# Two ends of an attention kernel written as lists of single-engine steps, with all leaf sums of weights on GpSimd

## The chip, the cores and the metric

The kernel runs on one core of a Trainium2 chip. The metric is the device time of one execution in microseconds. The kernel before took 1024.07 us, the median of 3 runs (1023.55 to 1025.17).

## The reference

The inputs are 64 blocks of 128 tokens with 512 channels in float32, a mask, a bias for each of 16 heads and the weights. What is computed is attention with one shared key/value head, a layer norm ahead of it and one behind it, and a residual:

```
xn   = layernorm(x, g_in)
q    = (xn @ Wq) * 64**-0.5        # 16 heads of 64
k, v = split(xn @ Wkv)             # one head of 64, shared
k, v = a null key and a null value (from cond) put in front of k and v
sim  = q k^T + bias, -max where the key is later than the query or masked
out  = softmax(sim) v              # joined to 1024 channels
x    = x + layernorm(out @ Wo, g_out)
```

## The kernel before

The instructions of each engine stand in the order in which the Python functions are called: the tile framework adds the semaphores, but moves nothing. Each engine takes its own queue in order, and so does SyncE (SP), which issues nearly all DMAs. So the order of the calls is the schedule.

The work goes in cycles of two blocks (`cycle(c)`, 28 of them, c from 2 to 29), each a fixed table of steps (`EVEN` and `ODD`). A cycle makes the q projection of blocks ahead, softmax and values of two blocks, and the output projection and layer norm of older ones. At its end `region_mm(c)` puts the scores of the next two blocks and the values of these two on TensorE. The scores of the first of the two go into the PSUM bank `s`, which the values need next: so TensorE waits there for VectorE to add the scores to the bias tile (`scores_add`, the rows `s<-ps,s`).

q projections and output projections are done with seven products instead of eight (sums of quarters of the operands are formed first); half of the q products go one level deeper. The sums of weights for that level are the "leaf sums": `leaf_weights(k, j)` for five leaves k and four sums j, 20 adds or subtracts of 128x256 elements in all, made once. The sums j = 1, 2 and 4 write a tile of their own (`wL`); j = 3 overwrites part of the weights (`wq` or `wS`), and so may only run once the products that need those weights are done. The table of cycle 2 is the first to use them.

Ahead of cycle 2 stands a part written by hand: loads, the norm of the first 16 blocks, scaling of `wq` by the gain (`weights_q`), the transposes of tokens on TensorE (`norm_T`, tile `pxT`), q products of the first group in full (`q_half`, tile `pq`), the keys and values (`kv_mm`, `kv_out`, tile `kT`), a transposed copy of the values (`vt`, written by VectorE, sent to DRAM as `vd`), a DMA that copies the keys to the upper half of the partitions (`kT<-kT`), bias tiles on GpSimd (`bias_add`, 128x1552), then `region(-1)`, the first seven-product q projections (`q_one`), `region(0)`, and `second()`, which is cycle 1 and ends with `region(1)`. Nine leaf sums run on GpSimd there, eleven on VectorE: six in a row in `second()`, five of the kind that overwrites, in ones and twos, shortly ahead of `region(1)`.

Behind cycle 29 a second hand-written part finishes the last six blocks: `scores_lower`, `scores_upper`, `exps`, `scale`, `blocks_T` and `values_one` for blocks 60 to 63, three sets of seven output products (`out_one`), the last layer norms (`pair_stats`, `pair_center`, `pair_scale`) and the stores.

The calls that both VectorE stretches come from:

```
        for j in (1, 2, 4):
            leaf_weights(1, j, nc.vector)
            leaf_weights(5, j, nc.vector)
```

Of the kernel before, what the change touches and what calls it, by code (L numbers as in the profile page):

```python
# [17 lines left out]
def kernel(  # L18
# [63 lines left out]
    P = 128  # L82
# [236 lines left out]
    def norm_T(m):  # L319
        g, t = divmod(m, GB)  # L320
        if t == 0:
            xT[g] = gp.tile([P, GB, KC, N], FP, tag="xT", name=f"xT_{g}")
        xh = xs.pop(m)
        pt = ps_w.tile([P, KC, P], FP, tag="w", name=f"pxT_{m}")
        for kc in range(KC):
            nc.tensor.transpose(pt[:, kc, :], xh[:, kc * P : (kc + 1) * P], ident)
        nc.scalar.copy(xT[g][:, t], pt)

# [107 lines left out]
    def q_part(g, c, h):  # L436

        f = c % NF
        return qT[g, f // FH, h][:, f % FH, :, :, c // NF, :]

    def q_half(c, h, at=None):
        if c == 0 and h == 0:
            for fp in range(2):
                q_tile(0, fp)
        tag = at or ("XY"[c % 2] if h else "ac"[c % 2])
        pq = (ps_q if tag in "ac" else ps_y).tile([P, HT], FP, tag=tag, name=f"pq_{c}_{h}")
        two = slice(2 * h, 2 * h + 2)
        for kc in (2, 0, 3, 1):
            nc.tensor.matmul(
                pq,  # L450
                wq[:, kc, c * P : (c + 1) * P],
                xT[0][:, two, kc, :],
                start=(kc == 2),
                stop=(kc == 1),
            )
        nc.scalar.copy(
            q_part(0, c, h),
            pq.rearrange("p (t i q) -> p t i q", t=2, i=NQ),
        )

    def q_first(f, k, tag):

        pool = {"a": ps_q, "c": ps_q, "X": ps_y, "Y": ps_y, "s": ps_s, "w": ps_w}[tag]
        if f == 0 and k == 1:
            for fp in range(2):
                q_tile(0, fp)
        product(0, f, k, pool, tag, start=k in (1, 2, 5))
        o = {
            1: (f, 0),
            2: (f, 0),  # L470
            6: (f, 1),
            7: (HC + f, 1),
            4: (HC + f, 0),
            5: (HC + f, 1),
            3: (f, 1),
        }[k]
        o = q_part(0, *o)
        if k in (2, 3, 5):
            nc.vector.tensor_tensor(o, by_block(tag), o, ALU.add)
        else:  # L480
            nc.scalar.copy(o, by_block(tag))
# [469 lines left out]
    def out_sum(p, k):  # L951

        if k == 0:
            yS[p] = bp.tile([P, HC, N], FP, tag="yS", name=f"yS_{p}", bufs=1)
        h11, h12 = oT[p][:, lo_c], oT[p][:, hi_c]
        h21, h22 = oT[p + 1][:, lo_c], oT[p + 1][:, hi_c]
        o, l, m, op = (
            (yS[p], h21, h22, ALU.add),
            (h11, yS[p], h11, ALU.subtract),
            (h21, h22, h11, ALU.subtract),  # L960
            (h12, h12, h11, ALU.subtract),
        )[k]
        nc.gpsimd.tensor_tensor(o, l, m, op)  # L963

    def out_product(p, k, pool, tag, start=True):
        key = "y" + tag
        if start:
            prod[key] = pool.tile([P, HE], FP, tag=tag, name=f"py{tag}_{p}_{k}")
        a, b = oT[p], oT[p + 1]
        h, w = {  # L970
            1: lambda: (a[:, lo_c], e11),
            2: lambda: (a[:, hi_c], e21),
            3: lambda: (a[:, hi_c], e22),
            4: lambda: (b[:, hi_c], wT[:, 2]),
            5: lambda: (yS[p], wT[:, 0]),
            6: lambda: (a[:, lo_c], wT[:, 1]),
            7: lambda: (b[:, lo_c], e12),
# [122 lines left out]
    def q_one(c, k, h):  # L1100
        i = 2 * c + 4 + h
        g, f = divmod(i, GB)
        if k == 1 and f % FH == 0:
            q_tile(g, f // FH)
        if k == 1:
            product(g, f, 1, ps_q, "a")
            keep("a", "p1")
        elif k == 2:
            product(g, f, 2, ps_w, "w")
            q_out(g, f, lo_t, "w", "p1")  # L1110
        elif k == 5:
            product(g, f, 5, ps_q, "c")
        elif k == 6:
            product(g, f, 6, ps_q, "a", start=False)
            keep("a", "u2")
        elif k == 7:
            product(g, f, 7, ps_q, "a", start=False)
            keep("a", "u3")
            q_out(g, HC + f, hi_t, "c", "u3")
        elif k == 3:  # L1120
            product(g, f, 3, ps_q, "c", start=False)
            q_out(g, f, hi_t, "c", "u2")
        else:
            product(g, f, 4, ps_q, "a", start=False)
            q_out(g, HC + f, lo_t, "a")

# [22 lines left out]
    def out_one(p, k, dve=False):  # L1149
        if k == 3 and at_end:  # L1150
            out_add(p, 3)
        out_mm(p, k)
        if k in (1, 6, 7) or (k == 4 and not at_end):
            out_copy(p, k, dve)
        if k == 4 and at_end:
            out_part(p + 1, 0, "w", "yu3")
        elif k == 3 and at_end:
            o = y_half(p, 1)
            nc.vector.tensor_tensor(o, prod["yw"], o, ALU.add)
        elif k in (2, 3, 7):  # L1160
            out_add(p, k)

# [8 lines left out]

    def region(c):
        n0, n1 = 2 * c + 2, 2 * c + 3
        region_mm(c)
        scores_add(n0, 1)
        scores_add(n0, 0)
        if c < 0:
            scores_max(n0, 0)
            scores_max(n0, 1)
        scores_add(n1, 0)  # L1180
        scores_add(n1, 1)

    def key_values(m):
        if m < B:
            kv_out(m, kv_mm(m))

    def second():
        b0, b1, n0, n1 = 2, 3, 4, 5
        p, m = 0, 12
        load_mask(2)  # L1190
        load_x(m)
        values_out(p, (0, 2))
        scores_max(b1, 0)
        scores_max(b1, 1)
        values_out(p + 1, (0, 2))
        scores_max(b0, 0)
        tokens_in(2)
        q_one(1, 1, 0)
        q_one(1, 5, 0)
        values_out(p, (1, 3))  # L1200
        values_out(p + 1, (1, 3))
        out_sum(p, 0)
        scores_max(b0, 1)
        q_one(1, 2, 0)
        exps(b0, 0, 0, 2)
        q_one(1, 6, 0)
        exps(b0, 0, 2, 8)
        out_one(p, 1)
        mask_neg(1)
        out_sum(p, 1)  # L1210
        for j in (1, 2, 4):
            leaf_weights(1, j, nc.vector)
            leaf_weights(5, j, nc.vector)
        rinv(b0, 0)
        q_one(1, 7, 0)
        out_one(p, 2)
        exps(b0, 1, 0, 6)
        norm_stats(m)
        q_one(1, 4, 0)
        load_x(m + 1)  # L1220
        q_one(1, 3, 0)
        scale(b0, 0)
        q_one(1, 1, 1)
        q_one(1, 2, 1)
        exps(b0, 1, 6, 8)
        exps(b1, 0, 0, 6)
        norm_stats(m + 1)
        rinv(b0, 1)
        scale(b0, 1)
        key_values(8)  # L1230
        out_sum(p, 3)
        q_one(1, 6, 1)
        exps(b1, 0, 6, 8)
        norm_apply(m)
        out_sum(p, 2)
        exps(b1, 1, 0, 4)
        tokens_T(m)
        out_one(p, 6)
        rinv(b1, 0)
        q_one(1, 5, 1)  # L1240
        exps(b1, 1, 4, 8)
        load_x(m + 2)
        nc.tensor.addr_align(256, offset=120, max_nops=16)
        scale(b1, 0)
        token_sum(2, 1)
        token_sum(2, 2)
        out_one(p, 5)
        norm_apply(m + 1)
        blocks_T(b0)
        rinv(b1, 1)  # L1250
        q_one(1, 7, 1)
        tokens_T(m + 1)
        out_one(p, 7)
        scale(b1, 1)
        q_one(1, 3, 1)
        blocks_T(b1)
        out_one(p, 4)
        bias_add(n0)
        leaf_weights(3, 3, nc.vector)
        load_x(m + 3)  # L1260
        load_res(p + 1)
        q_one(1, 4, 1)
        leaf_weights(4, 3, nc.vector)
        bias_add(n1)
        out_one(p, 3)
        leaf_weights(2, 3, nc.vector)
        leaf_weights(1, 3, nc.vector)
        leaf_weights(5, 3, nc.vector)
        load_res(p)
        leaf_sums(2, 1)  # L1270
        leaf_sums(2, 5)
        region(1)
# [419 lines left out]


    nc.vector.tensor_scalar(gin8, gin, DH**-0.5, None, ALU.mult)
    keep_busy(14)
    load_second()
    norm_stats(0)
    norm_stats(1)
    norm_apply(0)
    norm_T(0)  # L1700
    norm_apply(1)
    for kc in (2, 0, 3, 1):
        weights_q(kc, 0)
    norm_T(1)
    keep_busy(2)
    causal()
    norm_stats(2)
    norm_stats(3)
    norm_apply(2)
    norm_apply(3)  # L1710
    q_half(0, 0)
    weights_kv()
    weights_q(2, 1)
    q_half(1, 0)
    norm_T(2)
    weights_q(3, 1)
    norm_T(3)
    load_x(11)
    weights_q(0, 1)
    norm_stats(4)  # L1720
    weights_q(1, 1)
    norm_stats(5)
    q_half(2, 0)
# [319 lines left out]
```

## Time and profile before

| | |
|---|---|
| median of 3 runs | 1024.07 us |
| profiled execution, its own time | 1022.62 us |
| its span, first to last instruction | 1020.8 us |
| TensorE (PE) busy | 1002.5 us, 98% |
| VectorE (DVE) busy | 908.3 us, 89% |
| GpSimd (POOL) busy | 834.8 us, 82% |
| ScalarE (ACT) busy | 677.6 us, 66% |
| mean granted TensorE clock | 0.996 |

TensorE is busy for almost the whole span, so only its idle time, and time at a lower clock, can be saved without taking work away. A timeline row reads: start in us, duration in us, engine, line, operation, out<-in, shape, and in brackets the idle time before it with what ended it. In a row with several instructions (x4) the duration is that of the whole stretch. Ends of matmuls are modelled, so from row to row the starts are what tells. A table by stretches gives busy time and, as PEclk, the share of the full TensorE clock that was granted.

### The profile page before, as it was taken

To read this page: it belongs to the slowest core of one execution; us is meant where nothing else is said; L and a number is where in the kernel's file an instruction comes from. 1 tells how busy PE (TensorE), PEld (TensorE's weight loads), DVE (VectorE), ACT (ScalarE), POOL (GpSimd) and SP (SyncE) were. 2 spreads that over 40 slices of the span, in tenths; PEclk is the share of its full clock that TensorE was granted. 3 is DMA by queue.
4 is the path that set the end of the run, shared out by engine and by line. 5 is a ranking of instruction groups with operands and counts; after the bars stand their busy time and mean duration, and the time that the engine had idled before them with its cause. 6 is when DMAs were issued, how large, how long until landed. Compare 5 with 4: busy or idle time off the path is not lost. (4 is left out here: it accounts for less than half of the span.)

```text
span 1020.8 us, 32742 instructions
## 1 busy us (share of the span) xinstructions
PE 1002.5 (98%) x12440; PEld 901.8 (88%) x12440; DVE 908.3 (89%) x2151; ACT 677.6 (66%) x2826; POOL 834.8 (82%) x819
## 2 busy tenths in 40 slices
PE   9998999999999999999999999999999999999997
PEld 8887899999999999999999999999999999999876
DVE  7787899898998989999898998989999898888898
ACT  2654766668766668766668766668766668756591
POOL 3798879789797997979789796997979789696874
PEclk9999999999999999999999999999999999999999
DMA  6541242333424325342333424325342332421212
GB/s 220 158 128 32 61 120 85 105 88 105 128 83 130 86 64 138 94 120 84 106 88 104 129 82 127 85 69 137 96 119 84 107 86 84 119 65 43 73 34 103
DMA packets 70293, 101.37 MB, mean 99 GB/s; under 512 B 27744, under 2 KB 31328, under 8 KB 68320
## 3 DMA queue, kind: packets, MB, share of 16 engines
q1 hardware_dynamic: 69008, 97.83, 34.1%
q8 instruction: 123, 2.02, 0.9%
q10 hardware_dynamic: 1104, 1.05, 0.3%
q14 instruction: 58, 0.48, 0.2%
HBM read 63.19 MB, written 33.55 MB: 95 GB/s over the span
## 5 line engine op out<-in xcount | busy, mean ns | idle before, releaser
L821 ACT ACTIVATE s<-s,nmax 128x129 f32<-128x129 f32 (+1 forms) x1024 | 374.7, 377 | 3.5 <-DVE nmax L812 3.5
L755 POOL TENSOR_TENSOR s<-biasp,mneg 128x1552 f32<-128x1552 f32 x64 | 206.0, 3232 | 11.7 <-DVE sb L857 9.8
L842 POOL TENSOR_TENSOR s<-s,rinv 128x512 f32<-128x512 f32 (+1 forms) x128 | 188.4, 1481 | 23.2 <-DVE rinv L838 21.5
L821 ACT ACTIVATION_READ_ACCUMULATOR s<-s,nmax 128x1 f32 x1024 | 205.4, 201 | 0.0
L576 DVE TENSOR_TENSOR qT<-pl,qT 128x128 f32<-128x128 f32 (+1 forms) x420 | 127.6, 331 | 43.3 <-PE pl L573 38.3
L930 ACT ACTIVATE oT<-poY,nv 128x256 f32<-128x256 f32 x58 | 29.2, 503 | 202.9 <-PE poY L890 190.8
L807 DVE TENSOR_TENSOR s<-ps,s 128x256 f32<-128x256 f32 (+2 forms) x224 | 122.3, 599 | 15.1 <-PE ps L771 14.6
L980 PE MATMUL pyX<-wo,oT 128*128 128x256 f32 x512 | 121.6, 380 | 0.5 <-ACT kyu L1013 0.5
L812 DVE TENSOR_REDUCE nmax<-s 128x8 f32<-128x1032 f32 (+1 forms) x128 | 119.9, 949 | 0.1
L980 PE MATMUL pyX<-wT,oT 128*128 128x256 f32 x488 | 115.6, 380 | 0.7 <-POOL oT L963 0.7
L857 DVE STREAM_TRANSPOSE sb<-s 128x1536 f32<-128x1536 f32 x64 | 112.6, 1759 | 1.8 <-POOL s L842 1.8
L963 POOL TENSOR_TENSOR yS<-oT 128x512 f32<-128x512 f32 x32 | 41.0, 1281 | 82.4 <-ACT oT L930 81.6
L980 PEld LDWEIGHTS pyX<-wo,oT 128*128 128x128 f32 x512 | 92.7, 190 | 12.1 <-issue 1.1
L980 PEld LDWEIGHTS pyX<-wT,oT 128*128 128x128 f32 x488 | 88.3, 190 | 10.9 <-POOL oT L963 1.1
L771 PE MATMUL ps<-kT,qT 64*64 64x128 f32 (+1 forms) x4096 | 93.7, 245 | 0.7 <-issue 0.7
L771 PEld LDWEIGHTS ps<-kT,qT 64*64 64x64 f32 x4096 | 85.6, 134 | 5.8 <-issue 2.4
L890 PE MATMUL pos<-sb,vr 32*64 32x128 f32 (+1 forms) x1792 | 82.1, 324 | 4.1 <-DVE s L807 3.9
L890 PE MATMUL poY<-sb,vr 32*64 32x128 f32 x720 | 75.3, 351 | 0.0
L890 PE MATMUL poX<-sb,vr 32*64 32x128 f32 x960 | 74.4, 302 | 0.0
L980 PE MATMUL pyw<-wo,oT 128*128 128x256 f32 x280 | 66.4, 380 | 0.1
L890 PEld LDWEIGHTS pos<-sb,vr 32*64 32x64 f32 x1792 | 60.8, 131 | 4.8 <-DVE s L807 4.2
L890 PEld LDWEIGHTS poX<-sb,vr 32*64 32x64 f32 x960 | 56.2, 132 | 5.9 <-issue 5.2
(180 smaller groups left out, 2681.3 us busy)
## 6 DMA issues: line engine op xcount, KB each, us to landing
res<-in_x_dram SPq DMA_DIRECT2D x64, 256.0 KB, 3.0
out_dram<-y SPq DMA_DIRECT2D x58, 256.0 KB, 2.1
x<-in_x_dram SPq DMA_DIRECT2D x224, 64.0 KB, 2.0
xd<-xb SPq DMA_DIRECT2D x14, 1024.0 KB, 4.6
xT<-xd SPq DMA_DIRECT2D x56, 256.0 KB, 6.3
vr<-vd SPq DMA_DIRECT2D x64, 128.0 KB, 3.6
x<-in_x_dram SPq DMA_DIRECT2D x8, 256.0 KB, 4.9
vd<-vt SPq DMA_DIRECT2D x32, 64.0 KB, 4.2
```

Source lines behind the costliest of these rows:

```text
L576: nc.vector.tensor_tensor(o, p, o, ALU.add)
L755: nc.gpsimd.tensor_tensor(S[b], biasp, mneg[:, t].unsqueeze(1).broadcast_to([P, R8, ROW]), ALU.add,)
L771: nc.tensor.matmul(to[r][i * DH : (i + 1) * DH, f, :], qT[g, f // FH, t // GH][rows, f % FH, t % GH, NQ - 1 - i if hf else i], kT[g][rows, ...
L807: nc.vector.tensor_tensor(sv, ps, sv, ALU.add)
L812: nc.vector.tensor_reduce(nmax[b][:, hf], S[b][:, :, WITH_NULL[hf]], AX.X, ALU.max, negate=True)
L821: nc.scalar.activation(row, row, AF.Exp, bias=nmax[b][:, hf, k : k + 1], accum_out=rsum[b][:, hf, k : k + 1],)
L842: nc.gpsimd.tensor_tensor(sv, sv, rinvs.pop((b, hf)).unsqueeze(2).broadcast_to([P, R8, sv.shape[2]]), ALU.mult,)
L857: nc.vector.transpose(sb.rearrange("p j e q -> p e j q"), S[b][:, :, 1 : ROW - 1].rearrange("p e (j k) -> p e j k", k=Q),)
L890: nc.tensor.matmul(po[s][rows, half], vr[g][quad(s), j, t, :], sb[quad(s), slots, r * NF : (r + 1) * NF, :], start=start, stop=True, skip_ ...
L930: nc.scalar.activation(o, pos[b][s], AF.Identity, bias=nv2)
L963: nc.gpsimd.tensor_tensor(o, l, m, op)
L980: nc.tensor.matmul(prod[key], h[:, c, :], w[:, c, :], start=(start and c == 0), stop=(c == HC - 1), skip_group_check=not start,)
```

## The change

Both hand-written parts become lists of steps, `FRONT` (from the first norm to the end of cycle 1) and `TAIL` (from cycle 29 to the end), run through a table of functions `act`. Helpers that issued to several engines are split, so that each step belongs to one engine: `q_half` becomes `qh` (products) and `qhc` (copy), `norm_T` becomes `xTt` and `xTc`, `q_one` becomes `q`, `qk`, `qo` and `qc`, the `exps` go in twos, the output copies of values one by one. The order of all steps is new. The instructions are the same in kind and number, but for these: all 20 leaf sums are issued to GpSimd (the argument `on` is never given), fewer address alignments of TensorE's instructions (two ahead of cycle 2 in place of five), and tiles of q are taken when first written. The tables of cycles 2 to 29 are unchanged.

```diff
-    def q_half(c, h, at=None):
...
-        for j in (1, 2, 4):
-            leaf_weights(1, j, nc.vector)
-            leaf_weights(5, j, nc.vector)
...
-        leaf_weights(3, 3, nc.vector)
...
-        leaf_weights(4, 3, nc.vector)
...
-        leaf_weights(2, 3, nc.vector)
-        leaf_weights(1, 3, nc.vector)
-        leaf_weights(5, 3, nc.vector)
...
+        if (g, f // FH, h) not in qT:
+            q_tile(g, f // FH)
...
+    FRONT = (
+        ("busy", 2),
...
+        ("lw", 1, 1),
...
+        ("stats", 7),
...
+        ("kvc", 0),
...
+        ("wq", 3, 1),
...
+        ("wq", 2, 1),
...
+        ("vT", 0),
...
+        ("vsend", 0),
...
+        ("ksend", 0),
...
+        ("region", -1),
...
+        ("lw", 4, 3),
+        ("qc", 1, 4, 1),
+        ("ocopy", 0, 4),
+        ("region", 1),
+        ("apply", 13),
+        ("lsum", 2, 1),
+        ("addS", 4, 1),
+        ("addS", 5, 0),
+        ("lsum", 2, 5),
...
+    TAIL = (
...
+        ("scale", 63, 1),
...
+        ("osum", 60, 2),
+        ("rinv", 63, 0),
+        ("voutV", 62, 0),
+        ("out", 60, 5),
+        ("scale", 63, 0),
...
+        ("blocksT", 63),
...
+        ("store", 62),
+        ("olast", 62, 4),
+        ("store", 57),
+        ("part", 63, 0),
+        ("store", 56),
+        ("pstats", 63),
+        ("center", 63),
+        ("ppow", 63),
+        ("pscale", 63),
+        ("store", 63),
+    )
...
+        "lw": leaf_weights,
...
+    for name, *args in FRONT:
+        act[name](*args)
     for c in range(LEAF, B // 2 - 2):
         cycle(c)
     at_end.append({})
+    for name, *args in TAIL:
+        act[name](*args)
```

**VectorE in cycle 1, before.** `mneg` is the mask, `wL<-` are leaf sums, `rinv` a reciprocal of the softmax, and the last row adds the kept product to the one in PSUM bank `c` (`pc`), which frees that bank for TensorE's next product.

```order
L745 TENSOR_SCALAR mneg<-m_1_185 128x4x64
L745 TENSOR_SCALAR mneg<-m_1_185 128x4x128
L529 TENSOR_TENSOR wL<-wq 128x256
L529 TENSOR_TENSOR wL<-wS 128x256
L529 TENSOR_TENSOR wL<-wL,wq 128x256
L529 TENSOR_TENSOR wL<-wL,wS 128x256
L529 TENSOR_TENSOR wL<-wq,wL 128x256
L529 TENSOR_TENSOR wL<-wS,wL 128x256
L838 RECIPROCAL rinv_0_999<-rsum_971 128x8
L737 TENSOR_TENSOR qT_1_1_952<-pc_2_5_957,kept 128x8x32
```

The same place with the change:

```order
L687 TENSOR_TENSOR qT_1_1_978<-pc_2_5_973,kept 128x8x32
L695 TENSOR_SCALAR mneg<-m_1_185 128x4x64
L695 TENSOR_SCALAR mneg<-m_1_185 128x4x128
L687 TENSOR_TENSOR qT_1_1_978<-pc_2_5_973,kept 128x8x32
L788 RECIPROCAL rinv_0_1051<-rsum_931 128x8
L807 STREAM_TRANSPOSE sb_1064<-s_764 128x8x6x32
```

The six leaf sums no longer stand ahead of the rows that free bank `c`.

**VectorE ahead of region(1), before.** `sb<-s` is the transposed softmax of a block, `wS<-wS` and `wq<-wq` are leaf sums that overwrite, the last row adds the scores of block 4 and frees the bank that the values wait for.

```order
L857 STREAM_TRANSPOSE sb_1142<-s_747 128x8x6x32
L529 TENSOR_TENSOR wS<-wS 128x2x128
L529 TENSOR_TENSOR wq<-wq 128x2x128
L1005 TENSOR_TENSOR y_1010<-pyY_5_1113,kyu_1091 128x256
L529 TENSOR_TENSOR wq<-wq 128x2x128 x2
L529 TENSOR_TENSOR wS<-wS 128x2x128
L807 TENSOR_TENSOR s_1149<-ps_1_1184,s_1149 128x8x128
```

With the change:

```order
L807 STREAM_TRANSPOSE sb_1134<-s_782 128x8x6x32
L955 TENSOR_TENSOR y_1114<-pyY_5_1093,kyu_1099 128x256
L368 TENSOR_SCALAR kT_1148<-pkv_1125,nkv 128x4x64
L687 TENSOR_TENSOR qT_1_1_978<-pc_3_5_1054,kept 128x8x32
L302 TENSOR_SCALAR nmr_1151<-mv_990,rstd_992 128x1
L757 TENSOR_TENSOR s_1089<-ps_1_1159,s_1089 128x8x128
```

Between the last transpose and the scores' add no leaf sum is left.

**VectorE near the start, before.** `st` is the statistics of a block (with its two small successors `mv` and `rstd`), `wq<-wq,gin` scales 512 columns of one quarter of `wq`; the q products of columns 512 and up (`pq` of the second half of `wq`) need all four such rows of that half.

```order
L1093 TENSOR_SCALAR wq<-wq,gin_83 128x512 x3
L284 BN_STATS st_300<-x_157 128x6
L286 BN_AGGR mv_302<-st_300 128x2
L288 TENSOR_SCALAR rstd_304<-mv_302 128x1
L1093 TENSOR_SCALAR wq<-wq,gin_83 128x512
```

With the change (the first two of the second half stand further up):

```order
L284 BN_STATS st_274<-x_159 128x6
L286 BN_AGGR mv_276<-st_274 128x2
L288 TENSOR_SCALAR rstd_278<-mv_276 128x1
L239 COPY nbp<-nbh 32x8 x4
L695 TENSOR_SCALAR mneg<-m_0_167 128x4x64
L695 TENSOR_SCALAR mneg<-m_0_167 128x4x128
L284 BN_STATS st_316<-x_163 128x6
L286 BN_AGGR mv_318<-st_316 128x2
L288 TENSOR_SCALAR rstd_320<-mv_318 128x1
L368 TENSOR_SCALAR kT_331<-pkv_252,nkv 128x4x64
L1043 TENSOR_SCALAR wq<-wq,gin_83 128x512
L302 TENSOR_SCALAR nmr_335<-mv_276,rstd_278 128x1
```

One more scaling row follows. The last two scalings moved behind the statistics of two more blocks, the null columns (`nbp`), the mask and the first write of `kT`. Further down, the transposed copy of the values (`vt`) moved from ahead of the `biasp` rows (`null_shift`) to behind them, and with it the three SyncE issues that follow it, the copy of the keys last.

More of the change, by code (lines that the diff above doesn't have):

```diff
@@ L317, in norm_apply @@
             )
[L319 to L327, printed above, removed]
     xbs = {}
@@ L438, in q_part @@
         f = c % NF
+        if (g, f // FH, h) not in qT:
+            q_tile(g, f // FH)
         return qT[g, f // FH, h][:, f % FH, :, :, c // NF, :]
-    def q_half(c, h, at=None):
[L442 to L481, printed above, removed]
     def weight_sum(k):
@@ L1098, in weights_kv @@
         )
[L1100 to L1125, printed above, removed]
     def out_mm(p, k):
@@ new lines, with q_half_mm @@
+    pq, pk, pt = {}, {}, {}
+    banks = {}
+    def q_half_mm(c, h):
+        tag = "XY"[c % 2] if h else "ac"[c % 2]
+        pq[c, h] = (ps_y if h else ps_q).tile([P, HT], FP, tag=tag, name=f"pq_{c}_{h}")
+        two = slice(2 * h, 2 * h + 2)
+        for kc in (2, 0, 3, 1):
+            nc.tensor.matmul(
+                pq[c, h],
+                wq[:, kc, c * P : (c + 1) * P],
+                xT[0][:, two, kc, :],
+                start=(kc == 2),
+                stop=(kc == 1),
+            )
@@ new lines, in q_half_out, with q_mm, q_keep @@
+    def q_half_out(c, h):
+        nc.scalar.copy(
+            q_part(0, c, h),
+            pq[c, h].rearrange("p (t i q) -> p t i q", t=2, i=NQ),
+        )
+    def q_mm(c, k, h):
+        g, f = divmod(2 * c + 4 + h, GB)
+        pool, tag = (ps_w, "w") if k == 2 else (ps_q, "c") if k in (3, 5) else (ps_q, "a")
+        product(g, f, k, pool, tag, start=k in (1, 2, 5))
+        if k == 2:
+            pt[c, h] = prod["w"]
+    def q_keep(c, k, h):
+        keep("a", {1: "p1", 6: "u2", 7: "u3"}[k])
@@ new lines, in value_step, with out_step @@
+    def value_step(b, k, n):
+        if n not in banks:
+            banks[n] = value_banks(n, True)
+        values_one(b, k, banks[n])
+    def out_step(p, k):
+        (out_last_mm if at_end else out_mm)(p, k)
+    act = {
+        "stats": lambda m: norm_stats(m, False),
+        "pow": norm_pow,
+        "nmr": norm_nmr,
+        "apply": norm_apply,
+        "xTt": tokens_transpose,
+        "xTc": tokens_copy,
+        "tokT": tokens_T,
+        "tok_out": tokens_out,
+        "tok_in": tokens_in,
+        "wq": weights_q,
+        "wkv": weights_kv,
+        "wsum": weight_sum,
+        "lw": leaf_weights,
+        "ows": out_weight_sum,
+        "tsum": token_sum,
+        "lsum": leaf_sums,
+        "busy": keep_busy,
+        "causal": causal,
+        "nullc": null_columns,
+        "nulls": null_shift,
+        "mneg": mask_neg,
+        "bias": bias_add,
+        "qh": q_half_mm,
+        "qhc": q_half_out,
+        "q": q_mm,
+        "qk": q_keep,
+        "qo": q_add,
+        "qc": q_copy,
+        "kv": kv_step,
+        "kvc": lambda m: kv_out(m, pk.pop(m)),
+        "vT": values_T,
+        "vsend": values_send,
+        "ksend": keys_send,
+        "vfetch": values_fetch,
+        "region": region_mm,
+        "lower": lambda *bs: scores_lower(bs),
+        "upper": lambda b, tags: scores_upper(b, ps_s if tags == "s" else ps_w, tags),
+        "addS": scores_add,
+        "smax": scores_max,
+        "exps": exps,
+        "rinv": rinv,
+        "scale": scale,
+        "blocksT": blocks_T,
+        "value": value_step,
+        "vout": lambda b, s: values_out(b, (s,)),
+        "voutV": lambda b, s: values_out(b, (s,), True),
+        "osum": out_sum,
+        "out": out_step,
+        "ocopy": lambda p, k: out_copy(p, k),
+        "ocopyV": lambda p, k: out_copy(p, k, True),
+        "oadd": lambda p, k: (out_add if not at_end or k == 7 or (k == 3) else out_last_add)(p, k),
+        "oadd3": out_last_add,
+        "olast": out_last_add,
+        "part": stats_part,
+        "pstats": pair_stats,
+        "ppow": pair_pow,
+        "center": pair_center,
+        "pscale": pair_scale,
+        "gain": gain_copy,
+        "xload": load_x,
+        "mask": load_mask,
+        "late": load_late,
+        "nullv": load_null_value,
+        "res": load_res,
+        "store": store,
+        "align": lambda offset: nc.tensor.addr_align(256, offset=offset, max_nops=16),
+    }
```

1002 lines of the change are left out of this document (579 added, 423 removed).

## The prediction

> **What bounds the kernel now.** I read TensorE in stretches first (us, busy time and rows, granted clock, DMA share, GB/s), since it is busy for 98% of the span:
>
> ```profile
> ...
> 70.00:80.00 10.00, 7.55 (x36) 1.00 0.53 130
> ...
> 100.00:110.00 10.00, 6.07 (x127) 0.83 0.10 29
> 110.00:950.00 840.00, 840.00 (x10607) 1.00 0.36 98
> 950.00:1010.00 60.00, 57.61 (x798) 1.00 0.22 71
> 1010.00:1020.80 10.80, 3.85 (x18) 0.81 0.26 101
> ```
>
> Between 110 and 950 nothing can be won: no idle time, full clock, and the tables there are unchanged. What there is to win is 2.45 us in 70–80, 3.93 in 100–110, 2.39 in 950–1010, and what lies around the last products. Then the list of TensorE's waits, which names the first two:
>
> ```profile
> PE pos L890 <- DVE s L807: 3.9, 1, 3.9
> PE pc L622 <- DVE qT L737: 2.5, 1, 2.5
> ```
>
> Then VectorE's timeline at both places (start, duration), to see why it was late:
>
> ```profile
> 72.77 0.95 DVE L529 TENSOR_TENSOR wL<-wq 128x256 f32<-128x256 f32 x1
> ...
> 79.17 0.37 DVE L737 TENSOR_TENSOR qT<-pc,kept 128x256 f32<-128x256 f32 x1
> ...
> 96.14 1.74 DVE L529 TENSOR_TENSOR wS<-wS 128x256 f32<-128x256 f32 x1
> 97.81 3.43 DVE L529 TENSOR_TENSOR wq<-wq 128x256 f32<-128x256 f32 x1
> ...
> 101.49 1.00 DVE L529 TENSOR_TENSOR wq<-wq 128x256 f32<-128x256 f32 x2
> ...
> 103.01 1.21 DVE L807 TENSOR_TENSOR s<-ps,s 128x1024 f32<-128x1024 f32 x1
> ```
>
> Both stalls are leaf sums. From 72.77 to 79.1 six of them stand ahead of the row that frees bank `c`; from 96.14 to 103 five of them stand ahead of the scores' add that frees the bank for the values. The same kind of sum takes 0.50 alone (101.49, two in 1.00) and up to 3.43. GpSimd's timeline shows what ran beside it:
>
> ```profile
> 94.36 6.59 POOL L755 TENSOR_TENSOR s<-biasp,mneg 128x1552 f32<-128x1552 f32 x2
> ```
>
> The slow sum ends at 101.24, the second of these two at 100.95: an add on VectorE waited for the whole GpSimd add.
>
> **The change part by part.** The sum is made against the profiled execution's 1022.62 us (span 1020.8); the median shown, 1024.07, is 1.45 above it.
>
> *Stalls removed.* In the new order no leaf sum stands ahead of either row. Idle 2.45 + 3.93 = 6.38. The clock: 0.83 over the ten microseconds behind the second stall is 1.7 us of full-speed work lost; the first stall, 2.45 long, left it at 1.00. If no stall of that length returns, 1.7 comes back. Together **−8.1**. The cover needed is VectorE free when the banks are done: in the new order only masks, statistics and q rows, each below 0.7, stand near them.
>
> *New waits near the start.* The last two scalings of `wq` move back. Rows that carry their costs:
>
> ```profile
> 15.08 0.69 DVE L284 BATCH_NORM_STATS2 st<-x 128x6 f32<-128x512 f32 x1
> ...
> 16.09 0.48 DVE L1093 TENSOR_SCALAR wq<-wq,gin 128x512 f32<-128x512 f32 x1
> ...
> 18.37 0.62 DVE L745 TENSOR_SCALAR mneg<-m 128x256 f32<-128x256 uint8 x2
> ...
> 21.02 1.23 DVE L490 TENSOR_TENSOR wS<-wS,wq 128x1024 f32<-128x1024 f32 x1
> ...
> 22.26 0.71 DVE L390 STREAM_TRANSPOSE vt<-kT 64x512 f32<-64x512 f32 x1
> ...
> 24.96 0.68 DVE L239 COPY nbp<-nbh 32x8 f32<-32x8 f32 x4
> ...
> 26.80 2.72 DVE L248 SCALAR_TENSOR_TENSOR biasp<-biasp,nbp,later 128x192 f32<-128x192 f32 x8
> ```
>
> A set of statistics takes 1.01 (15.08 to 16.09). Block 4's set would start at 14.66, one scaling (0.42) earlier than now; behind it three sets 3.03, the null columns and mask 1.4, the keys' write 0.40, two scalings and a small row 1.0: the last scaling ends at 20.0 to 20.5, where it ended at 16.57. TensorE has two products, the keys, two products and two transposes ahead of the one that needs it:
>
> ```profile
> 9.34 3.72 PE L449 MATMUL pq<-xT,wq 128*128 128x256 f32 x16 [0.23 <-ACT xT L327]
> ...
> 33.10 2.91 PE L771 MATMUL ps<-kT,qT 64*64 64x128 f32 x128
> ```
>
> The row of 3.72 is two products, with the last matmul's end in it: a pitch of 1.75. Five of them and 0.5 for each set of transposes, from 9.34 on, bring it there at about 19, so it waits 1 to 1.5, and everything behind it on TensorE with it.
>
> Then the keys. Their copy to the upper partitions is issued by SyncE behind the two `vd` issues, and these wait for `vt`, which moves behind all `biasp` rows. (Behind them in SyncE's queue stand token loads of later blocks.) From 20.0: two sets of statistics 2.0, three sums of `wq` at 1.24, eight `biasp` rows 2.7, a write of `kT` 0.40, small rows 0.4, `vt` 0.72, and 0.3 for waits: `vt` ends at 30.2, where it ended at 22.97.
>
> ```profile
> 24.69 1.33 SPq L399 DMA_DIRECT2D vd<-vt  x2
> 26.07 0.63 SPq L405 DMA_DIRECT2D kT<-kT  x1
> DMA to landing us min/median/max: 2.3/3.3/4.3
> ```
>
> 1.38 for the two issues and 2.4 from issue to landing (near the minimum, my choice): keys at 34.0, at the maximum 35.9. One product of 1.75 moves behind the first scores, so TensorE is there at 33.10 − 1.75 = 31.4 without any wait. Loss 2.6 in all (the wait for `wq` is inside it), between 0, if VectorE is 2.6 earlier than I add up, and 4.5. Behind it the new order leaves banks to be freed by rows that stand one or two later: no row of before shows these waits; from below nothing, from above one q-row's 0.41 each for four of them; I take 0.55 as between. Together **+3.15**; the queue behind the waiting product is the whole of TensorE, nothing of which can pass.
>
> *GpSimd.* It takes eleven sums more. Its load now:
>
> ```profile
> 9.30:29.60 20.30, 4.78 (x9) 1.00 0.63 184
> 29.60:105.20 75.60, 68.11 (x52) 1.00 0.35 100
> L529 POOL TENSOR_TENSOR wL<-wq,wL 128x256 f32<-128x256 f32 x2 | 1.8, 908 | 0.0
> L529 POOL TENSOR_TENSOR wL<-wq 128x256 f32<-128x256 f32 x2 | 1.5, 736 | 0.0
> 104.73 0.46 POOL L554 TENSOR_TENSOR xS<-xS,xL 128x128 f32<-128x128 f32 x1
> 107.74 1.22 PE L668 MATMUL pa<-xT,wq 128*128 128x128 f32 x4
> 109.24 0.61 PE L668 MATMUL pc<-xS,wS 128*128 128x128 f32 x4
> ```
>
> It is idle for 15.5 of the first 20.3 us, where seven of the twenty sums now go; 13 are left behind 28.5, before 9, so four more at 0.74 to 0.91: 3.4. 68.11 + 3.4 + some 2.5 of waits from 28.5 end at 102.4, where the last row now ends at 105.2. Cycle 2 uses that row 1.5 us after its start (107.74, 109.24), that is at 104.3 with a start moved by −8.1 + 3.15 to 102.8. Cost nothing, with 1.9 us to spare; if it were gone, each further microsecond would be one of TensorE's.
>
> *Tail.* VectorE is the engine there, TensorE waits for it:
>
> ```profile
> 964.77:1017.77 53.00, 50.56 (x99) 0.99 0.23 76
> 992.25 0.19 ACT L821 ACTIVATION_READ_ACCUMULATOR s<-s,nmax 128x1 f32 x1
> 994.56 2.01 DVE L1075 SCALAR_TENSOR_TENSOR y<-y,rstdo,res 128x512 f32<-128x512 f32 x1
> 998.13 1.77 DVE L857 STREAM_TRANSPOSE sb<-s 128x1536 f32<-128x1536 f32 x1
> 1017.02 0.75 DVE L1075 SCALAR_TENSOR_TENSOR y_end<-yc,rstdo,res 128x512 f32<-128x512 f32 x1
> out_dram<-y_end SPq DMA_DIRECT2D x6, 256.0 KB, 2.0
> res<-in_x_dram SPq DMA_DIRECT2D x64, 256.0 KB, 3.0
> ```
>
> The last exponentials end at 992.25, the last transpose of them starts only at 998.13. The new order has one of the two scalings of block 63 ahead of other GpSimd work, so that the transpose could start up to 4.4 earlier; but VectorE is idle for only 2.44 us, and a row slowed beside GpSimd (2.01 against 0.75 for the same line at 1017.02) holds 1.3 more. Gain at most 3.7. Costs: the residual of block 58 is loaded behind a row that VectorE must do first, and 3.0 + 0.4 stand against some 2.8 in which it has other rows (an estimate from rows of 0.4 to 0.75): 0.6. Two stores of 256 KB now stand between the last two: 0.5. As VectorE's work stays the same in kind and number, I take the gain as 2.3, near its idle time, net **−1.2**, with +1 and −3.5 as ends.
>
> Sum: −8.1 + 3.15 − 1.2 = −6.15; I take −5.9 for further small waits in cycle 1. 1022.62 − 5.9 = 1016.7; plus 1.45: **1018.2 us** as a median.
>
> **The rivals.**
>
> *GpSimd becomes the bound (slower).* Five of the moved sums are of the overwriting kind, which no GpSimd row of before shows. If they pay on GpSimd what the worst paid on VectorE, waiting there for whole VectorE adds, 3.43 in place of 0.9, GpSimd ends at 102.4 + 5 × 2.5 = 114.9. From 104.3 on that stalls cycle 2, from 109.2 on it makes the kernel slower: +5.7, with the tail 1028.6. Against it: six leaf shapes at 0.74 to 0.91, and no VectorE add but 1.24 long to wait for. Chance 0.08. The Trainium skill ("SBUF — State Buffer", section "Who interferes with whom") states this exclusion: a VectorE add with two SBUF inputs and a GpSimd instruction reading SBUF block each other for the whole instruction. The pair of ends at 101.24 and 100.95 agrees; that GpSimd pays likewise, no row here shows.
>
> *The early part gives it back.* Keys land after 4.3 (4.5 lost), further waits of 2 behind it as softmax shifts: front −1.6, tail 0: 1022.5. For it: `vt` 7 us later. Against it: TensorE has q products that could fill, though its order is fixed. Chance 0.15, half of it within 0.2%.
>
> *No early loss, tail in full.* VectorE runs ahead near the start as much as I add waits: −8.1 − 3.5 = −11.6: 1012.5. For it: VectorE's waits at the start are guesses. Against it: the rows moved ahead of `vt` are real work. Chance 0.12.
>
> **How the numbers follow.** The forecast has 0.65, its own range 1014.5 to 1021.5. The range for 8 in 10 reaches down to 1013.0, just short of the third rival, and up to 1023.5, where it holds most of the second; the first lies outside. What a measurement can tell is about 0.2%, 2 us: faster is below 1022.0: 0.61 of the forecast's 0.65, all of the third rival's 0.12 and 0.05 of the second's 0.15, 0.78 together; within 0.2% the forecast's other 0.04, 0.08 of the second and 0.01 of the first, 0.13; slower 0.07 of the first and 0.02 of the second, 0.09.
>
> **What would show it.** The rows of TensorE waiting for `pc` and `pos` gone, clock 1.00 in 95–110; first scores at about 34, waiting for the keys' copy; the last `xS<-xS,xL` on GpSimd ending near 102.4 and cycle 2 starting near 102.8; the last `sb<-s` at 996 or so. Wrong: a new wait over 2 us in cycles 1 or 2, GpSimd's last row behind 105, or residuals and stores holding the tail's end.

## The result, and the profile after

The changed kernel takes 1017.59 us (median of 4 runs, 1017.02 to 1017.79), beside 1023.98 us (1023.55 to 1025.17, 4 runs) for the kernel before: ratio 0.9935, 95% interval 0.9918 to 0.9952, or 6.7 us less (4.9 to 8.4). Its profiled execution took 1017.74 us with a span of 1015.9. TensorE by stretches (us, busy time and rows, granted clock, DMA share, GB/s):

```profile
10.00:70.00 60.00, 56.73 (x484) 1.00 0.39 117
70.00:80.00 10.00, 10.00 (x165) 1.00 0.75 213
80.00:100.00 20.00, 20.00 (x129) 1.00 0.25 57
100.00:110.00 10.00, 10.00 (x247) 1.00 0.46 132
...
940.00:1005.00 65.00, 61.78 (x826) 1.00 0.19 59
1005.00:1015.90 10.90, 5.08 (x24) 0.85 0.38 144
```

From 70 to 110 nothing is idle and the clock is full: both stalls and the slow stretch are gone. What is new is 3.27 us of idle time in 10–70, where there had been 0.69. TensorE's waits name it (engine, line, what it waited for: total, times, longest; the row of `poa` lies in the tail, at 994, and that of `pq<-xT` ahead of 10 us, the other five make up 3.25):

```profile
PE pxT L2128 <- DVE kT L368: 1.7, 2, 1.2
...
PE poa L840 <- DVE sb L807: 1.3, 1, 1.3
...
PE pq L2082 <- ACT xT L2132: 0.7, 1, 0.7
...
PE ps L721 <- DMA kT<-kT: 0.5, 1, 0.5
PE pxT L2128 <- ACT xT L2132: 0.4, 1, 0.4
...
PE pq L2082 <- DVE wq L1043: 0.3, 1, 0.3
PE pq L2082 <- ACT qT L2091: 0.3, 1, 0.3
```

The largest is a transpose that needs a PSUM bank, and the bank holds the keys and values that VectorE has yet to copy out (`kT<-pkv`). Four places of TensorE's timeline (start, duration) mark the run: first scores (waiting for the keys' copy inside them), start of cycle 2, last product:

```profile
35.88 0.43 PE L721 MATMUL ps<-kT,qT 64*64 64x128 f32 x4
36.79 2.90 PE L721 MATMUL ps<-kT,qT 64*64 64x128 f32 x124 [0.48 <-DMA kT<-kT]
...
104.29 0.71 PE L618 MATMUL pa<-xT,wq 128*128 128x128 f32 x4
...
1008.19 1.89 PE L930 MATMUL pyw<-wT,oT 128*128 128x256 f32 x8
```

Four of the 128 matmuls of the first scores start at 35.88, the others at 36.79, which is where I take the first scores to be: 3.7 later than before. Cycle 2 is 3.45 earlier (107.74 to 104.29), the last product 3.77 earlier, the last VectorE row 4.83 earlier (its end 1017.77 to 1012.94). The last product before, then the last VectorE row with the change:

```profile
1011.96 1.89 PE L980 MATMUL pyw<-wT,oT 128*128 128x256 f32 x8
```

```profile
1012.19 0.75 DVE L1025 SCALAR_TENSOR_TENSOR y_end<-yc,rstdo,res 128x512 f32<-128x512 f32 x1
```

So of 4.9 us between the two profiles the front has 3.45, the cycles and the last products 0.3, and what comes behind the last product 1.06. The medians differ by 6.4. The 1.5 us between the two figures are a question of their own, which experiments 3, 9 and 10 take up.

### The profile page after: what moved, and what is told of

Its sections match the earlier page's. It is cut to its first block, busy times and chain, and to the rows that moved or that the text cites. A ratio compares the mean times of both kernels' runs of the same rounds, so it can differ in the third digit from the quotient of the medians.

```text
span 1015.9 us, 32646 instructions
## 1 busy us (share of the span) xinstructions
PE 1001.3 (99%) x12440; PEld 900.2 (89%) x12440; DVE 895.5 (88%) x2140; ACT 679.9 (67%) x2826; POOL 842.4 (83%) x830
## 5 line engine op out<-in xcount | busy, mean ns | idle before, releaser
L792 POOL TENSOR_TENSOR s<-s,rinv 128x1024 f32<-128x1024 f32 (+1 forms) x128 | 187.9, 1478 | 21.9 <-DVE rinv L788 20.2
L880 ACT ACTIVATE oT<-pos,nv 128x256 f32<-128x256 f32 x124 | 53.0, 482 | 14.2 <-PE pos L840 14.2
```

The source lines that it names most:

```text
L792: nc.gpsimd.tensor_tensor(sv, sv, rinvs.pop((b, hf)).unsqueeze(2).broadcast_to([P, R8, sv.shape[2]]), ALU.mult,)
L880: nc.scalar.activation(o, pos[b][s], AF.Identity, bias=nv2)
```

## The experiments

The same places in all profiles, with the time of each against the kernel before in its own runs (the starts are of TensorE's rows; "cycle 2" is its first product; in the changed kernel and in 2, four scores stand 0.91 ahead of the start given):

| kernel | first scores | cycle 2 | last product | span | median, us | ratio (95%) |
|---|---|---|---|---|---|---|
| before | 33.10 | 107.74 | 1011.96 | 1020.8 | 1023.7 to 1024.4 | 1 |
| changed | 36.79 | 104.29 | 1008.19 | 1015.9 | 1017.59 | 0.9935 (0.9918–0.9952) |
| 1 leaf sums on GpSimd, old order | 33.49 | 100.43 | 1007.01 | 1015.9 | 1017.21 | 0.9935 (0.9922–0.9947) |
| 2 changed front only | 37.55 | 105.16 | 1008.96 | 1017.8 | 1018.83 | 0.9951 (0.9939–0.9964) |
| 3 changed tail only | 33.19 | 110.54 | 1013.36 | 1021.1 | 1022.11 | 0.9980 (0.9972–0.9989) |
| 4 changed, early keys | 36.73 | 104.72 | 1007.86 | 1015.6 | 1017.08 | 0.9932 (0.9918–0.9945) |
| 5 = 1 + changed tail | 33.22 | 100.28 | 1006.54 | 1014.3 | 1016.12 | 0.9921 (0.9909–0.9934) |
| 6 = 5 + five sums early | 33.92 | 103.51 | 1009.31 | 1017.1 | 1018.83 | 0.9950 (0.9937–0.9962) |
| 7 = 4 + early power | 34.77 | 103.54 | 1007.33 | 1015.1 | 1016.87 | 0.9931 (0.9918–0.9945) |
| 8 = 5 + four sums moved | 33.40 | 100.44 | 1004.55 | 1012.3 | 1014.15 | 0.9909 (0.9895–0.9922) |
| 9 five sums on GpSimd | 33.34 | 103.03 | 1009.36 | 1018.2 | 1020.15 | 0.9970 (0.9959–0.9980) |
| 10 six sums on GpSimd | 33.16 | 105.44 | 1009.47 | 1018.3 | 1020.45 | 0.9970 (0.9960–0.9981) |

### 1. The leaf sums alone, in the old order

```diff
     values_send(0)
+    leaf_weights(1, 1)
+    leaf_weights(1, 2)
...
     keys_send(0)
+    leaf_weights(5, 1)
...
     weight_sum(4)
+    leaf_weights(5, 2)
+    leaf_weights(5, 4)
...
     weight_sum(3)
+    leaf_weights(1, 4)
...
-        for j in (1, 2, 4):
-            leaf_weights(1, j, nc.vector)
-            leaf_weights(5, j, nc.vector)
...
-        leaf_weights(3, 3, nc.vector)
+        leaf_weights(3, 3)
...
```

(and so for the other four of `j = 3`)

> The kernel before, with nothing changed but the leaf sums: all eleven go from VectorE to GpSimd. Six stand near the start or behind the first scores, the five that overwrite stand where they stood. Theory A (the two stalls and the slower clock behind them are what the front has to win, and GpSimd has room): 8.1 us less, about 1016.0. Theory B (GpSimd becomes the bound at cycle 2): in the changed kernel its last row ahead of cycle 2 ends at 103.6, and cycle 2 uses it 1.0 us after its start, so cycle 2 starts at 102.6 at the earliest in place of 107.74: at most 5.1 us less, about 1019, with a TensorE wait at the start of cycle 2. If the sums on GpSimd cost far more than 0.73 each there, no gain.

Cycle 2 starts at 100.43, 7.31 us earlier. Of the 8.1 of stalls and clock, 0.54 lay behind the start of cycle 2 before (the clock was 0.50 from 107 to 108 and 0.59 from 108 to 109), so 7.56 could show there: the stalls were removed nearly in full. There TensorE then waits, as theory B has it. Its timeline at that place:

```profile
100.43 0.71 PE L668 MATMUL pa<-xT,wq 128*128 128x128 f32 x4
102.35 0.49 PE L668 MATMUL pa<-xL,wL 128*128 128x128 f32 x2 [1.21 <-POOL xL L554]
...
104.13 0.49 PE L668 MATMUL pc<-xL,wL 128*128 128x128 f32 x2 [0.62 <-POOL xL L554]
```

1.83 us of waits for GpSimd, and from cycle 2 to the last product 906.6 where it was 904.2. What is left is 4.95 at the last product; theory B had at most 5.1. The median, 1017.21, lies between the two theories' 1016.0 and 1019. With the sums alone moved, the old order and the old tail, the kernel is as fast as the changed one. The fair comparison for the new order of the front is experiment 2, which has the old tail too and ran beside the same runs of before: it takes 1018.83, and each of its times (1018.48 and up) is above each of these (1017.64 and down). So the moved sums carry the gain of the front, and its new order cost some 1.6 us.

### 2 and 3. Front and tail apart

2 against the changed kernel:

```diff
-    for name, *args in TAIL:
-        act[name](*args)
+    values_fetch(NG - 1)
+    scores_lower((B - 2, B - 1))
...
```

(the old tail, to its end), and 3 against the kernel before, with the functions that `TAIL` calls:

```diff
-    values_fetch(NG - 1)
...
-    store(B - 1)
+    for name, *args in TAIL:
+        act[name](*args)
```

> The changed kernel with its front, and the last part of the kernel before. Cycle 2 starts 3.45 us earlier in the profile of the changed kernel (107.74 to 104.29), its last product 3.8. If front and tail add up, this one is 3.5 to 3.9 us faster than before: 1020.1 to 1020.5. If the tail gave nothing and the medians' whole 6.4 is the front's, it is at 1017.6.

> The kernel before with the changed last part. By the profile of the changed kernel the time from the last product's start to the last VectorE row falls from 5.81 to 4.75 us, and TensorE's part is no shorter: 1.0 us less, 1023.0. By the prediction's term 1.2 less, 1022.8. If the medians' 6.4 less the profile's 3.5 to 3.9 of the front is the tail's: 2.5 to 2.9 less, about 1021.3.

By the ratios the front is worth 5.0 us (3.7 to 6.2), the tail 2.0 (1.1 to 2.9): 7.0 together, beside the change's 6.7 (4.9 to 8.4). In the profile of 3 the last VectorE row ends 4.75 behind the start of the last product (5.81 before), as in the changed kernel, so the 1.06 are the tail's. That profile also shows what its span of 1021.1 hides. TensorE in four stretches behind the first stall and around the second:

```profile
80.00:85.00 5.00, 5.00 (x17) 0.66 0.00 0
...
100.00:105.00 5.00, 2.13 (x98) 0.95 0.01 2
105.00:110.00 5.00, 3.95 (x108) 0.50 0.02 3
110.00:115.00 5.00, 5.00 (x42) 0.86 0.37 105
```

The front is the same as before, and the idle times too (2.5 and 3.9 us). But here the first stall did lower the clock: 0.66 over five microseconds is 1.7 lost, where the profile of before shows 1.00. Behind the second stall the clock is at half for 6.8 us in place of 3.4, but 1.5 of these lie in the stall itself, which ends at 106.05, and cost nothing:

```profile
105.00:106.00 1.00, 0.00 (x0) 0.50 0.00 0
106.00:107.00 1.00, 0.95 (x34) 0.50 0.09 16
```

What is lost there is half of the other 5.3, that is 2.7 in place of 1.7. So the price of these stalls is not the same in each execution.

### 9 and 10. One stall removed at a time

9 leaves the six sums on VectorE and gives GpSimd the five of `j = 3`, each in its place:

```diff
-        leaf_weights(3, 3, nc.vector)
+        leaf_weights(3, 3)
...
```

10 has the other edits of experiment 1 and leaves these five:

```diff
-        for j in (1, 2, 4):
-            leaf_weights(1, j, nc.vector)
-            leaf_weights(5, j, nc.vector)
...
+    leaf_weights(1, 1)
+    leaf_weights(1, 2)
...
```

> The kernel before, with only the five overwriting leaf sums on GpSimd, where they stand; the six in a row stay on VectorE. The second stall (3.93) and the slower clock behind it (1.7) go, the first (2.45) stays. Theory A (the first stall leaves the clock alone): 5.6 less, 1018.3. Theory B (the first stall lowers the clock too in most executions, and is what sets the median of before above its profile): 4.2 or less, 1019.8, with a clock below 1.00 between 80 and 100 and times that spread over 2 us. GpSimd's 3.65 us more are no bound in either, since TensorE comes to cycle 2 at 102 or later.

> The kernel before, with only the six leaf sums of the row on GpSimd, near the start; the five overwriting ones stay on VectorE. The first stall (2.45) goes, the second (3.93) and the clock behind it stay. Theory A (the first stall leaves the clock alone): 2.45 less, 1021.5. Theory B (it lowers the clock in most executions): 3.5 to 4 less, 1020.0 to 1020.5, and times that spread less than those of before.

In 9 the profiled execution has the first stall (2.42) and a clock of 1.00 behind it:

```profile
80.00:85.00 5.00, 5.00 (x24) 1.00 0.00 0
```

Its eight times fall into two groups, 1019.86 to 1020.30 (five) and 1021.36 to 1021.55 (three), some 1.4 apart, close to the 1.7 that the lowered clock cost in 3. The mean clocks do not tell the groups of 9 apart (0.998 to 0.999 and 0.997 to 0.998; they hold the time behind the last product as well). So neither theory held as it stood: the first stall lowers the clock in some executions, three of eight here if the groups are that, which is not shown. The second stall alone (10) has two groups as well, 1020.12 to 1020.45 with a mean clock of 0.996 to 0.997 and 1021.10 to 1021.31 with 0.994 to 0.995. Its median is as theory B has it; by the ratio, 3.1 us less than before (1.9 to 4.1), it cannot be told from either. The fourteen runs of before beside them reach from 1022.61 at a clock of 0.996 to 1025.73 at 0.993. That the groups are the two outcomes is inferred, in 10 from times and mean clocks and in 9 from times alone; only the profile of 3 shows a lowered clock behind the first stall directly. Nor are these stalls the only source of spread: experiments 5 and 6, which have neither, reach from 1014.90 to 1017.24 and from 1018.07 to 1020.20, with a mean clock of 0.999 at the fast end and 0.997 at the slow one.

In 9 GpSimd holds TensorE back too (1.12 and 0.61 at cycle 2), against what I wrote for it: TensorE arrived at 103.03, and GpSimd's sums, put where VectorE's had stood, end later still. These 1.73 us are in the median of 1020.15 too, which so does not decide between the theories' 1018.3 and 1019.8.

```profile
103.03 0.71 PE L668 MATMUL pa<-xT,wq 128*128 128x128 f32 x4
104.87 0.49 PE L668 MATMUL pa<-xL,wL 128*128 128x128 f32 x2 [1.12 <-POOL xL L554]
```

### 4 and 7. Mending the start of the new order

```diff
+        ("kvc", 0),
+        ("wq", 3, 1),
+        ("wq", 2, 1),
         ("stats", 5),
...
         ("kv", 2),
+        ("kvc", 2),
+        ("vT", 0),
+        ("vsend", 0),
+        ("ksend", 0),
```

and on top of it, in 7:

```diff
         ("stats", 4),
...
+        ("pow", 4),
         ("kvc", 0),
         ("wq", 3, 1),
         ("wq", 2, 1),
+        ("nmr", 4),
         ("stats", 5),
```

The moved steps no longer stand where they stood.

> The changed kernel with seven steps near the start moved: the first two blocks' key and value rows, the last two scalings of wq and the transposed values with their sends stand as early on VectorE as their inputs allow. The profile of the changed kernel shows 3.25 us of TensorE idle between its first q product and the first scores, 1.75 of it waiting for those key rows, 0.35 for the scalings, 0.48 for the keys' copy. Theory A (this loss is real and carried to the end): 2 to 3 us faster than the changed kernel, 1014.6 to 1015.6. Theory B (GpSimd, whose last row ahead of cycle 2 ends 0.7 us before cycle 2 begins, binds next): 1.7 us at most unless its rows move too. Theory C (the wait only moves to another row of the start): no change, 1017.6.

> The fourth experiment (early keys in the changed kernel) with two steps more: the power and the scale row of block 4 stand directly behind its statistics, not behind the power of block 5 and the eight GpSimd rows that make the causal mask. In the fourth experiment TensorE waited 2.56 us for a copy on ScalarE queued behind block 4's norm, which waited for these. Theory A (the early loss lies in this chain): that wait gone, first scores at about 34 in place of 36.7, 1015 to 1015.5 unless GpSimd holds cycle 2 back (then 1016). Theory C (it moves on again): no change, 1017.1.

In 4 the wait moved on, to a ScalarE copy queued behind the norm of block 4:

```profile
23.81 0.66 PE L2128 MATMUL pxT<-ident,x 128*128 128x128 f32 x4 [2.56 <-ACT xT L2132]
...
36.73 2.91 PE L721 MATMUL ps<-kT,qT 64*64 64x128 f32 x128
```

Theory C of the three. In 7 that wait is gone and first scores start 2.0 earlier than in the changed kernel, but cycle 2 only 0.75, with waits of 0.31 and 0.59 for VectorE between; another wait of 1.77 at the start took the old one's place:

```profile
25.07 1.99 PE L2082 MATMUL pq<-xT,wq 128*128 128x256 f32 x8 [1.77 <-ACT qT L2091]
27.80 1.13 PE L2128 MATMUL pxT<-ident,x 128*128 128x128 f32 x8 [0.73 <-ACT x L315]
```

By the ratio neither can be told from the changed kernel. The early loss is real, but it is no single late row: with the products in this order, ScalarE's copies, VectorE's rows and GpSimd's powers are all just in time or late there. Why only 0.75 of the 2.0 arrived, I did not take further.

### 5, 6 and 8. Can both kernels be beaten?

5 is the edits of 1 and 3 together. 6 adds to it, with the five calls taken from where they stood:

```diff
     leaf_weights(5, 1)
     null_columns()
+    leaf_weights(4, 1)
...
     q_half(4, 0)
+    leaf_weights(4, 2)
+    leaf_weights(2, 1)
     null_shift(0, R8)
     norm_nmr(7)
+    leaf_weights(4, 4)
...
     leaf_weights(5, 4)
+    leaf_weights(3, 1)
```

8 adds to 5, in their place, two early sums and two of the overwriting kind where GpSimd waited:

```diff
     norm_stats(7)
     q_half(4, 0)
+    leaf_weights(4, 1)
+    leaf_weights(2, 1)
     null_shift(0, R8)
...
         q_one(1, 2, 1)
+        leaf_weights(1, 3)
+        leaf_weights(2, 3)
...
```

> The first experiment (leaf sums on GpSimd in the old order) with the changed last part added. Theory A (leaf sums carry the front's gain, and the tail adds its own 1 to 2.3): 1015.0 to 1016.2, faster than the changed kernel, that is, the new order of the front has no part in the gain. Theory B (the parts overlap: what the tail gains is lost once the front is earlier): 1017.2, as the first experiment.

> The one above with five more leaf sums (the first of block 2, three of block 4, the first of block 3) taken from 46 to 76 us to the idle time that GpSimd has between 25 and 40. In the first experiment TensorE waited at the start of cycle 2 for GpSimd, 1.21 and 0.62 us. Theory A (GpSimd's load behind the first scores bounds it): five sums of 0.73 less there, the 1.83 us of waits gone: 1.8 less than the one above, about 1013.5 to 1014.5. Theory B (GpSimd waits there for others, its load is no bound): no change against the one above.

> The fifth experiment (leaf sums on GpSimd in the old order, changed last part) with four sums moved: one of block 4 and one of block 2 to the gap ahead of the first bias tiles, where GpSimd idles 4 us, and two of the overwriting kind (blocks 1 and 2) behind the last product that reads their weights, near 82, where GpSimd waited 0.85 for VectorE. Theory A (GpSimd's load between the first bias tile and cycle 2 is the bound, as long as room is also made where it waits): the 1.7 us that TensorE waits at the start of cycle 2 fall by about 1.4: 1014.7. Theory B (every row put ahead of the bias tiles comes back later, as in the sixth experiment): 1016 to 1018.

5 came out at 1016.12, as theory A has it, if at its upper end; its slowest time, 1017.24, lies among the changed kernel's, and the intervals of the two ratios overlap. 6 is 2.7 slower than 5, against both of its theories. TensorE's waits in it:

```profile
45.08 1.13 PE L622 MATMUL pc<-xS,wS 128*128 128x256 f32 x4 [1.15 <-POOL xS L504]
47.28 1.13 PE L622 MATMUL pa<-xS,wS 128*128 128x256 f32 x4 [1.07 <-POOL xS L504]
...
105.39 0.49 PE L668 MATMUL pa<-xL,wL 128*128 128x128 f32 x2 [1.17 <-POOL xL L554]
```

GpSimd takes its queue in order, and one of the early sums waited 1.57 us for VectorE's `wS`, with the token sums behind it that TensorE needs at 45. The two bias tiles started later too, behind the early sums (32.38 in 6, 30.15 in 5). Of the 3.65 that five sums take, 0.57 was left at 76, and that was idled away further on, where GpSimd waited 4.5 for VectorE (0.85 in 5):

```profile
81.27 0.55 POOL L295 TENSOR_TENSOR rstd<-rstd,nhalf 128x1 f32<-128x1 f32 x1 [2.58 <-DVE rstd L288]
84.79 0.55 POOL L295 TENSOR_TENSOR rstd<-rstd,nhalf 128x1 f32<-128x1 f32 x1 [1.95 <-DVE rstd L288]
```

8 uses that: it makes room early and fills the gap late. The wait of 1.08 to 1.21 at cycle 2 is gone, that of 0.61 stays, and the last product starts 2.0 earlier than in 5 (1006.54 there):

```profile
100.99 0.49 PE L668 MATMUL pa<-xL,wL 128*128 128x128 f32 x2
...
102.76 0.49 PE L668 MATMUL pc<-xL,wL 128*128 128x128 f32 x2 [0.61 <-POOL xL L554]
...
1004.55 1.89 PE L980 MATMUL pyw<-wT,oT 128*128 128x256 f32 x8
```

Only 1.1 of these 2.0 are won at cycle 2: the next product with `xL` starts at 104.81 there, at 105.91 in 5. The other 0.9 comes behind it, where the two kernels are the same, and where the profiles of the kernels with the new tail differ by as much as 1.6 (899.05 in 3 to 900.63 in 5, from that product to the last). So the profile shows 1.1 for the moved sums.

The time is 1014.15 us, ratio 0.9909 (0.9895 to 0.9922), 9.3 us less than before (8.0 to 10.8), with the old order of the front; theory A had 1014.7. Each of its four times (1013.81 to 1015.07) is below all of the changed kernel's, and the runs of before beside the two differ by 0.3 in their medians. By the ratios 8 is 1.2 us below 5, which is not clear of the noise.

## Why the prediction was right, and where its terms were off

The time was forecast at 1018.2 and came at 1017.59, in the likeliest case's own range. Two of its terms were off, by 1.0 and by 1.6 us, in opposite directions: the mechanism was right, but that the sum came within 0.6 of the median is in part luck.

**Stalls removed, −8.1: right.** Both waits are gone, the clock is 1.00 in 70–110. The first experiment shows 7.31 of the 7.56 that could show at cycle 2, its first scores 0.39 later.

**New waits near the start, +3.15: too small, and by another path.** Cycle 2 at 104.29 is 4.1 behind 107.74 − 7.56 = 100.18, where the sum had 3.15 and 0.25 more for small waits in cycle 1. The keys' copy was forecast to land at 34.0, at the latest 35.9; the first scores stand at 36.79. The step from issue to landing held (2.46 against 2.4). `vt` was late:

```profile
32.23 0.71 DVE L380 STREAM_TRANSPOSE vt<-kT 64x512 f32<-64x512 f32 x1
34.33 0.63 SPq L395 DMA_DIRECT2D kT<-kT  x1
```

It ends at 32.94, not 30.2. My sum had 0.3 of waits on VectorE; there were 0.45 and 1.13 for GpSimd's powers, an add of 1.62 in place of 1.22 and a `biasp` row of 0.88 in place of 0.41, both beside adds on GpSimd. And the keys were the smaller part: only 0.48 of the waits is theirs, 1.75 is for PSUM banks that VectorE's key rows free, which I had not followed. The wait for the scalings was 0.35 by name, not 1 to 1.5, since the transposes ahead of it already waited. What I had put behind the first scores, 0.55, did not show: there is no idle time from 37 on.

**GpSimd, nothing: right, with less margin.** The last row was forecast to end at 102.4 and ends at 103.58; cycle 2 came 1.5 later than forecast as well.

```profile
77.07 0.73 POOL L479 TENSOR_TENSOR wq<-wq 128x256 f32<-128x256 f32 x1
...
103.12 0.46 POOL L504 TENSOR_TENSOR xS<-xS,xL 128x128 f32<-128x128 f32 x1
```

The first rival's price, 3.43 for an overwriting sum on GpSimd, was 0.72 to 0.73. But GpSimd as the bound was there, by its load and not by that price: with TensorE 3.9 earlier, experiment 1 runs into it for 1.83 us. The loss at the start and the margin on GpSimd belong together: the new order arrives at cycle 2 when GpSimd is ready.

**Tail, −1.2: right in size (1.06 behind the last product; the 0.3 between cycle 2 and that product is less than the 0.54 of clock that the removed stall gives back there), wrong in place.** The last transpose of softmax did start earlier, 992.89 against 998.13, 1.5 beyond the general shift. TensorE made nothing of it: in the new order it comes to the products of this transpose before it is done, and waits for it.

```profile
992.89 1.77 DVE L807 STREAM_TRANSPOSE sb<-s 128x1536 f32<-128x1536 f32 x1
...
994.72 0.33 PE L840 MATMUL poa<-sb,vr 32*64 32x128 f32 x2 [1.30 <-DVE sb L807]
```

TensorE's idle time from 940 to 1005 is 3.2 us. What shortened is the part behind the last product, where one half of the last block's additions is now done before its end (the row of `pyY` at 1008.80; before, both halves came at 1014.43 and 1014.76). The stores, which I had priced at +0.5, cost nothing that shows: the span ends 3.0 behind the last VectorE row in both.

**From profile to median, +1.45: wrong.** By its own time the changed kernel was forecast at 1016.7 and took 1017.74. That error was made good by the offset that I carried over from before. The profile of before was a quick execution: its first stall had left the clock alone. Without the stalls that difference is not seen (profile 1017.74, median 1017.59), though experiment 5 shows that such a kernel can spread by 2.3 as well. That the offset is this clock rests on experiments 3, 9 and 10 and on the clocks of the runs of before; I have not seen it in a profile of before. As far as these runs show, the term that failed is thus the clock behind the stalls: 1.7 in the profile, more in the median execution.

**The second rival** (the early part gives it back) had the keys later than I had, but for another reason: its landing of 4.3 was 2.46, and `vt` was late. Of its front of 1.6 net, 4.0 came (8.1 less 4.1), nearer to my 4.95, and its tail of 0 was wrong. The third did not happen.

## What to carry to other kernels

When a stall is cured by moving work to another engine, try that move alone in the old order first; here it was worth as much as the whole change, the new order of the front cost 1.6 us beside it, and with the changed tail and four more moved rows the same move gave the shortest times measured. The bound that comes next is the engine that took the work: look where it idles in its queue, since room made ahead of such a wait is lost in the wait unless something fills it (6 against 8, though 6 also held up the token sums). And a time taken from one profile is not the median where a stall decides about the clock: compare the profile's own time to the runs, and ask whether the change removes what makes them differ.

## What the runs showed of the hardware

A TensorE idle time of 2.47 us was followed by a lowered clock in one profile (3, 0.66 over the next 5 us); 2.45 and 2.42 us left it at 1.00 in two others (before and 9), with the same program up to there. The Trainium skill ("TensorE: Matmul & The Clock Gate", section "What's actually happening") has the clock halved after an idle window of about 3.4 us that runs freely. The 1.7 us lost in 3 is 3.4 at half clock, which agrees; that 2.47 of idle time can be enough, the page does not lead one to expect.

VectorE and GpSimd seem to have held each other up in both directions. In the changed kernel two adds overlap, and both are long: on VectorE 1.62 for a shape that takes 1.22 at 29.90, on GpSimd 1.68 for one that takes 0.72 at 21.25:

```profile
22.05 1.68 POOL L479 TENSOR_TENSOR wL<-wL,wq 128x256 f32<-128x256 f32 x1
...
23.18 1.62 DVE L440 TENSOR_TENSOR wS<-wS,wq 128x1024 f32<-128x1024 f32 x1
```

Short waits seem to cost TensorE more than their length. From the first q product to the first scores the changed kernel takes 27.2 us for one product (1.75) less than before, which took 23.8: 5.2 more, of which 3.25 is idle time. The other 1.9, about 0.3 for each of six waits, is in longer rows beside them (1.97 to 1.99 in place of 1.89, and their pitch); this is worked out from starts, not measured by itself.
